# Layer starts of a four-layer graph kernel: first rows and values in banks of their own, transposes of two blocks first, accumulator banks reordered

## The chip, the core and the metric

The kernel runs on one core of one Trainium2 chip. The metric is device time in microseconds (us). Before the change it is 2941.99 us, the median of 3 runs (2940.94 to 2942.51).

A core has TensorE (PE in the profile, with its weight loads as PEld), VectorE (DVE), ScalarE (ACT), GpSimd (POOL) and SyncE (SP, which here only issues transfers). The engines run side by side and meet through semaphores. Matmul results land in PSUM, which has eight banks of 128 partitions by 512 fp32 values. Everything else lives in SBUF.

## The reference

4096 nodes with 256 features pass through four layers. Each is wrapped in `x = layernorm(x + layer(x, adj))`. The adjacency is symmetric with ones on the diagonal, about 1.6% dense.

```python
# layer 1: additive attention, 4 heads of 64
Wh = (h @ W).reshape(n, heads, d)
e = leaky_relu(s_i[:, None, :] + s_j[None, :, :], 0.2)      # s_i, s_j = Wh . a[:, :d], Wh . a[:, d:]
alpha = softmax(where(adj == 0, -inf, e), axis=1)
out = elu(einsum('ijh,jhd->ihd', alpha, Wh))
# layer 2: multi-head attention, 4 heads of 64
q, k, v = split(x @ Wq + bq), split(x @ Wk + bk), split(x @ Wv + bv)
attn = softmax(q k^T / 8 + (edge.T - 1) * 10000);  ctx = attn @ v
# layer 3: additive attention, one head, slope 0.01, elu(attention @ h)
# layer 4: cosine attention
att = softmax(where(adj > 0, cosine(x Wq^T, x Wk^T), -9e15));  out = 0.5 * att @ x + 0.5 * x
```

## The kernel before

All matmuls are fp32, and an fp32 matmul shows as two PE records. The 4096 query nodes are cut into 8 blocks `b` of QW = 512 (four tiles of 128 each), and the key nodes into 32 tiles `j` of 128 (layer 2: 64 half tiles of 64). The features of all nodes stay in SBUF, in `X`. Layer by layer, each unit (b, j) makes weights of 128 keys by 512 queries, and `sums` multiplies them by the values `V` into accumulators in PSUM. `transposed_block` (L112) turns the four tiles of a block of X by PE into `xT`, two banks of PSUM copied to SBUF.

**Layer 1** (`additive_heads`, L196). With `g = 1 - slope`, exp(leaky_relu(s_i + s_j)) is a factor times max(exp(g (s_i + s_j)), 1). So a unit needs a row of exp(g s_i), repeated on all partitions (`row`), and a column exp(g s_j) (`dst`). ScalarE does Relu(row x dst - 1) for each head (L255), VectorE adds 1 and multiplies by the mask (L256), and the sums (L266) follow two units behind (LAG = 2). The order on PE is written out by hand. At its head (L323 to L332) stand five warm-up matmuls, a product that spreads the vector `a` over all partitions for `attach` (L103, which adds the columns of s_i and s_j to the weights by VectorE), `turn(0)`, `prepare(0)` (L176: `V`, `src` and `dst` of block 0), `first_rows` (L228) and `turn(1)`. `first_rows` makes the first row by PE: four transposes per head of a broadcast column of `src`, each head's bank copied to `row[0]` in SBUF by VectorE or ScalarE in turn (L234). Two of its four banks are those of `side`, the others come from the pool `ga_ps` of two banks. PSUM is split into `ga_ps` (2 banks) and two accumulators `acc` of three banks; the first of them is `side`, used by every `prepare`.

**Layer 2** (`multi_head_attention`, L471). A prologue makes keys and queries (`keys`, L505, L510) and `values` (L517) of all blocks, in the order keys(0), the end of layer 1, then turn(b), values(b-1), keys(b); at the end values(6), `greatest` (L530) and values(7). `greatest` bounds the scores from the largest |q| and |k|; ScalarE's exp uses it as `shift`. The matmuls of `values` take 64 nodes at a time, and put the value halves of two pairs of heads on the lower and the upper 64 partitions of one bank, as `V` wants them (L524). VectorE adds the bias in two operations per block (L527). The prologue has one PSUM pool of eight banks. The main part takes them over: three tiles `p` of two banks for the scores (L578), and two accumulators. There PE, DVE and ACT follow a fixed order: scores, exp (L580), mask (L590), sums (L611) three units behind.

**Layer 3** (`additive_one`, L364) has one head and one column of weights per unit. Here a scheduler orders the engines by the program's order and the engines' readiness. `prepare` (L387) turns a block, makes its values (L176), and for the first two blocks the part of the row by transposes (L400) with a copy. Layer 2's last block is copied out of its accumulators (`kept`, L617) meanwhile. Accumulators of even blocks lie in `gb_pa`, of odd blocks (the last too) in the four banks of `gb_ps`.

**Layer 4** (`cosine_attention`, L779). `weights` multiplies normalised rows (L799, tile `p`), exp and mask follow (L802, L803), and `sums` (L810) add up two units behind. At the layer's start the end of layer 3 is still to come: `take_all` (L421, L424 to L426) empties its last accumulators, `outputs` finishes the rows, and `co.prepare` (L750: L761, L765, L767, L772, L776) makes the normalised rows of the last two blocks. PSUM pools come in the order `co_pz` (2 banks), `co_ps` (2), `co_pa` (4 accumulators), and take over the banks of layer 3 in that order.

Of the kernel before, what the change touches and what calls it, by code (L numbers as in the profile page):

```python
# [9 lines left out]
FP = mybir.dt.float32  # L10
# [18 lines left out]
def kernel(  # L29
# [82 lines left out]
    def transposed_block(sb, bank, b, copies=(nc.vector.tensor_copy, nc.scalar.copy)):  # L112

        xT = sb.tile([P, KC, QW], FP, name="xT")
        for c in range(KC):
            pt = bank()
            for k in range(QB):
                nc.tensor.transpose(pt[:, k * P:(k + 1) * P], X[:, b * QB + k, c * P:(c + 1) * P], ident)  # L118
            copies[c](xT[:, c, :], pt)
        return xT  # L120

# [74 lines left out]
    def additive_heads(a, H, slope, early, narrow, ahead):  # L196
# [7 lines left out]
        with ExitStack() as lay:  # L204
# [20 lines left out]
            def bank():  # L225
                return ps.tile([P, QW], FP, name="g")

            def first_rows():  # L228
                row[0] = rp.tile([P, H, QW], FP, name="row")
                for h in range(H):  # L230
                    pr = bank() if h % 2 else side[:, h, :]
                    for k in range(QB):
                        nc.tensor.transpose(pr[:, k * P:(k + 1) * P], src[:, k, h:h + 1].to_broadcast([P, P]), ident)
                    (nc.scalar.copy if h % 2 else nc.vector.tensor_copy)(row[0][:, h, :], pr)  # L234

            def rows(b, pr):

# [7 lines left out]
                nc.sync.dma_start(row[b].rearrange("p h i -> p (h i)"),  # L245
                                  far.rearrange("h k i -> (h k i)").unsqueeze(0).to_broadcast([P, H * QW]))

            def weights(b, j):
                m = b, j // MJ
                if j % MJ == 0:  # L250
                    mask[m] = mp.tile([P, MJ, QW], I32, name="mask")
                    nc.sync.dma_start(mask[m], edges[:, j:j + MJ, b * QW:(b + 1) * QW])
                z = prob[b, j] = zp.tile([P, H, QW], FP, name="prob")
                for h in range(H):
                    nc.scalar.activation(z[:, h, :], row[b][:, h, :], AF.Relu, bias=-1.0, scale=dst[:, j, h:h + 1])  # L255
                nc.vector.scalar_tensor_tensor(z, z, 1.0, mask[m][:, j % MJ, :].unsqueeze(1).to_broadcast([P, H, QW]),  # L256
                                               OP.add, OP.mult)

# [46 lines left out]
                    k = (j - 19) // 2  # L305
                    scale_row(X[:, b * QB + k, :D], mvs[b], roots[b][1], k)

            def turn(b):
                if b + 2 < NB:
                    load_x(b + 2)  # L310
                busy = (nc.scalar.copy if b == 0 else nc.vector.tensor_copy, nc.scalar.copy)
                xTs[b] = transposed_block(sb, bank, b, busy)

            def prepare(b):
# [5 lines left out]
            units = [(b, j) for b in range(NB) for j in range(NT)]  # L320
            with tc.manual_schedule(engines={mybir.EngineType.PE}):

                side = pa.tile([P, HC + 1, QW], FP, name="acc")  # L323

                for _ in range(5):
                    nc.tensor.matmul(side[:, 1, :P], ones, ones, start=True, stop=True)
                nc.tensor.matmul(side[:, 0, :], ones[:1, :], a_row, start=True, stop=True)
                attach(keep, w_sb, side[:, 0, :], H)
                turn(0)
                prepare(0)  # L330
                first_rows()
                turn(1)  # L332
                for i in range(len(units) + LAG):
                    if i < len(units):
                        b, j = units[i]
                        weights(b, j)
                        if (b, j) == (1, 4 * QB):
                            early()
                        if i % 8 == 4:
                            narrow(prob[b, j][:, 0, :1])  # L340
                    if i >= LAG:
                        b, j = units[i - LAG]
                        sums(b, j)
                        if b:
                            finish(b - 1, j)

                    if i == 0 or i % QB == 3 and 3 + i // QB <= NB:
                        b = 1 if i == 0 else 2 + i // QB
                        if b + 1 < NB:
                            turn(b + 1)  # L350
                        prepare(b)
                        if b == 3:
                            rows(1, bank())
                    if i == (NB - 1) * NT + 20:
                        ahead(bank)
# [8 lines left out]
    def additive_one(w_sb, slope, tail, op, follow):  # L364
# [3 lines left out]
        with ExitStack() as lay:  # L368
# [15 lines left out]
            def bank():  # L384
                return ps.tile([P, QW], FP, name="g")

            def prepare(b):  # L387
                xT = transposed_block(sb, bank, b)
                groups = [(k, 1, bank().rearrange("p (n f) -> p n f", n=1)) for k in range(QB)]
                additive_values(xT, b, groups, w_sb, V, src, dst, 1, slope)  # L390
                part = row[:, b * QW:(b + 1) * QW]
                if b > 1:

                    far = dr.tile([QB, P], FP, name="far")
                    nc.gpsimd.dma_start(far.rearrange("k p -> p k"), src[:, b * QB:(b + 1) * QB, 0])
                    nc.gpsimd.dma_start(part, far.rearrange("k p -> (k p)").unsqueeze(0).to_broadcast([P, QW]))
                    return
                pr = bank()
                for k in range(QB):
                    nc.tensor.transpose(pr[:, k * P:(k + 1) * P], src[:, b * QB + k, :].to_broadcast([P, P]), ident)  # L400
                nc.scalar.copy(part, pr)
# [31 lines left out]
                    layernorm_block(b, mvs[b])  # L433

            def even_bank():
                n = next(turn) % QB
                return pa.tile([P, QW], FP, name=f"acc{n}")

            prepare(0)
            prepare(1)  # L440
            turn = itertools.count()
            units = [(b, j) for b in range(NB) for j in range(NT)]
            for i in range(len(units) + 1):
                if i < len(units):
                    b, j = units[i]
                    weights(b, j)
                    if b == 0 and j % QB == 2 and j // QB + 2 < NB:
                        prepare(j // QB + 2)
                if i:
                    b, j = units[i - 1]  # L450
                    sums(b, j)
                    if (b, j) == (0, 2):
                        tail(bank)
                        follow.start()
                    if b and j % 4 == 0 and j // 4 < QB:
                        outputs(b - 1, j // 4)
                    if b == NB - 1 and j in (6, 10, 14):
                        follow.load_mask(0, (j - 6) // 4, prob[b, j][:, :1])

                    if b == NB - 1 and j % 4 == 2 and j // 4 < NB - 2:  # L460
                        follow.prepare(even_bank, j // 4)
                    if j == NT - 1:
                        take_all(b)
# [7 lines left out]
    def multi_head_attention(w_sb, b_sb, tail, rows_of_den, narrow_edges):  # L471
# [12 lines left out]
        with ExitStack() as lay:  # L484
# [7 lines left out]
            with ExitStack() as pro:  # L492
                wp = pool(pro, "mh_w", 1)
                sb = pool(pro, "mh_in", 3)
                ps = pool(pro, "mh_ps", 8, space=PSUM)
                big = {n: wp.tile([P, NB, KC], FP, name=f"{n}big") for n in "qk"}
                xTs = {0: b_sb["x"]}

# [16 lines left out]
                                                    apply_absolute_value=True)  # L515

                def values(b):  # L517
                    n = QW // d
                    for k in range(0, n, QB):
                        pv = bank().rearrange("p (k f) -> p k f", f=P)  # L520
                        for s in range(QB):
                            for c in range(KC):
                                for r in range(KC):
                                    nc.tensor.matmul(pv[r * d:(r + 1) * d, s, :], xTs[b][:, c, (k + s) * d:(k + s + 1) * d],  # L524
                                                     w_sb["v"][:, c, r * P:(r + 1) * P],
                                                     start=(c == 0), stop=(c == KC - 1))
                        nc.vector.tensor_tensor(V[:, b * n + k:b * n + k + QB, :], pv,  # L527
                                                b_sb["v"].unsqueeze(1).to_broadcast([P, QB, P]), OP.add)

                def greatest():  # L530

# [247 lines left out]
    def cosine_attention(co, tail):  # L779
        MJ = co.MJ  # L780
        T, in_ = co.T, co.pool
        with ExitStack() as lay:
            sb = pool(lay, "co_sb", 3)
            pz = pool(lay, "co_pz", 2, space=PSUM)
            ps = pool(lay, "co_ps", 2, space=PSUM)
            pa = pool(lay, "co_pa", 1, space=PSUM)
            ov = out.rearrange("(t p) d -> p t d", p=P)
            acc, prob, y = {}, {}, {}

# [78 lines left out]
    with ExitStack() as weights1, ExitStack() as den1, ExitStack() as weights3:  # L868
        wp = weights1.enter_context(tc.tile_pool(name="w1", bufs=1, side="right"))

        def early():
# [5 lines left out]
                bm_sb[n] = wp.tile([P, KC], FP, name=f"b{n}_sb")  # L877
                nc.sync.dma_start(bm_sb[n], bias)
            nc.vector.tensor_scalar_mul(bm_sb["q"], bm_sb["q"], (D // 4) ** -0.5)
            bm_sb["v"] = wp.tile([P, P], FP, name="bv_sb")  # L880
            for c in range(KC):
                half = slice(c * P // KC, (c + 1) * P // KC)
                nc.sync.dma_start(bm_sb["v"][half, :], bass.AP(tensor=bv1.tensor, offset=bv1.offset + c * P,
                                                               ap=[[0, P // KC], [1, P]]))
            load_w(w2_sb[:, :, :D], w2, nc.sync)
            attach(wp, w2_sb, spread(wp, a2, [[1, 2 * D]], [P, 2 * D], "a", nc.sync), 1)

# [51 lines left out]
```

## Time and profile before

The profiled execution spans 2938.2 us. Its chain of waits crosses from stage to stage at the following times; busy times of the engines within each stage come from the trace.

| stage | start to end, us | PE busy | DVE busy | ACT busy |
|---|---|---|---|---|
| layer 1 | 0 to 725.30 | 721.88 | 667.10 | 661.79 |
| layer 2, prologue | 725.30 to 819.95 | 93.48 | 43.81 | 31.59 |
| layer 2, main | 819.95 to 1730.22 | 904.42 | 702.41 | 566.17 |
| layer 3 | 1730.22 to 2251.23 | 519.23 | 288.43 | 237.21 |
| layer 4 | 2251.23 to 2938.20 | 676.55 | 240.11 | 171.75 |

Each row gives one stage; the difference between its length and the PE column is the time in which TensorE did nothing. Lines of the chain in order of time read: start in us, length in us, engine, tile, line of the kernel, and how many records. "issue" stands for time in which the profile shows nothing to wait for. A group line reads: line, engine, operation, out<-in with shapes, count, then total busy time and mean ns of one, then idle time before it and what ended it.

Of single kinds of work the trace shows: 16 additions L527 of 128x512, 690 ns each; the values' product L183 at 128x256 with 423 ns and at 128x768 with 954 ns; copies of xT (L119) of 128x512 by VectorE with 683 ns.

### The profile page before, as it was taken

The page shows a single profiled execution, that of the slowest core. Times are in us where ns is not written, and L with a number is a line of the kernel's source. Part 1 is how long each engine was busy: PE and PEld are TensorE (multiplying, and loading weights), DVE is VectorE, ACT ScalarE, POOL GpSimd, SP SyncE. Part 2 cuts the span into 40 slices and gives each one's busy share as a digit, 9 for nine tenths or more (in the row PEclk, how much of TensorE's full clock was granted, in tenths as well). Part 3 has the DMA queues.
Part 4 walks back from the last instruction along what each step waited for, and adds up shares of the span by engine and source line. Part 5 has one row for each costly group of instructions (what it writes and reads, how often), then busy time and mean ns, then how long its engine had stood idle before and what let it go on. Part 6 is the DMA issues. An engine that isn't in the chain of part 4 may idle for free.

```text
span 2938.2 us, 50968 instructions
## 1 busy us (share of the span) xinstructions
PE 2915.6 (99%) x20591; PEld 1564.9 (53%) x20591; DVE 1941.9 (66%) x2488; ACT 1668.5 (57%) x2606; POOL 927.5 (32%) x647
## 2 busy tenths in 40 slices
PE   9999999999999999999999999999999999999998
PEld 5333333333643333333333358888887777777776
DVE  8899999997467777877877865555555333333333
ACT  7899999997356666666666654444444222222222
POOL 1000010100078888888889860000000000000000
PEclk9999999999999999999999999999999999999999
DMA  7566666654068888889889876444442333333331
GB/s 202 104 136 142 136 137 139 142 128 80 1 146 191 184 182 190 179 186 192 176 189 187 179 160 139 151 151 151 154 132 53 50 58 58 58 58 58 58 58 29
DMA packets 207166, 374.91 MB, mean 128 GB/s; under 512 B 15073, under 2 KB 90833, under 8 KB 206034
## 3 DMA queue, kind: packets, MB, share of 16 engines
q0 software_dynamic: 102304, 177.77, 38.2%
q1 hardware_dynamic: 104352, 193.62, 20.2%
q8 instruction: 161, 2.64, 0.4%
q14 instruction: 75, 0.61, 0.1%
q10 hardware_dynamic: 274, 0.26, 0.0%
HBM read 317.00 MB, written 21.04 MB: 115 GB/s over the span
## 4 chain that ended last, share of the span: by engine, by line
PE 97%; DVE 2%; ACT 1%; issue 0%; DVEq 0%; ACTq 0%
PE acc L266 23%; PE acc L810 15%; PE p L578 14%; PE acc L611 14%; PE acc L418 8%; PE g L418 7%; PE p L799 4%; PE g L799 3%; PE g L510 2%; PE g L176 1%; PE g L524 1%; PE acc L176 1%; PE g L118 1%; PE acc L761 1%; DVE s L138 1%; DVE prob L590 1%
## 5 line engine op out<-in xcount | busy, mean ns | idle before, releaser
L590 DVE TENSOR_TENSOR prob<-p,mask 128x1024 f32<-128x1024 f32 x512 | 623.0, 1223 | 202.5 <-ACT p L580 198.3
L580 ACT ACTIVATE p<-p,shift 128x1024 f32<-128x1024 f32 x512 | 556.2, 1088 | 333.8 <-PE p L578 333.0
L266 PE MATMUL acc<-prob,V 128*32 128x512 f32 x6144 | 663.8, 592 | 0.0
L597 POOL TENSOR_TENSOR den<-den,prob 128x1024 f32<-128x1024 f32 x248 | 612.8, 2471 | 80.4 <-DVE prob L590 66.0
L255 ACT ACTIVATE prob<-row,dst 128x512 f32<-128x512 f32 x1024 | 635.5, 711 | 0.1
L256 DVE SCALAR_TENSOR_TENSOR prob<-prob,mask 128x2048 f32<-128x2048 f32 x256 | 582.8, 2287 | 25.1 <-ACT prob L255 21.5
L578 PE MATMUL p<-qT,kT 64*64 64x512 f32 x4096 | 532.7, 590 | 6.6 <-DVE prob L590 5.8
L611 PE MATMUL acc<-prob,V 64*64 64x512 f32 x4096 | 531.5, 589 | 0.0
L810 PE MATMUL acc<-X,prob 128*128 128x257 f32 x2048 | 485.7, 380 | 0.0
L810 PEld LDWEIGHTS acc<-X,prob 128*128 128x128 f32 x2048 | 388.5, 190 | 162.0 <-issue 114.7
L803 DVE TENSOR_TENSOR prob<-prob,mask 128x512 f32<-128x512 f32 x256 | 176.4, 691 | 420.1 <-ACT prob L802 418.9
L266 PEld LDWEIGHTS acc<-prob,V 128*32 128x32 f32 x6144 | 197.4, 110 | 451.6 <-issue 433.5
L91 POOL COPY tick<-prob 128x1 f32<-128x1 f32 x35 | 41.8, 1193 | 1016.8 <-DVE prob L256 643.7
L410 ACT ACTIVATE e<-row,dst 128x512 f32<-128x512 f32 x256 | 184.1, 721 | 235.4 <-DVE prob L412 208.4
L611 PEld LDWEIGHTS acc<-prob,V 64*64 64x64 f32 x4096 | 155.9, 133 | 285.3 <-issue 278.1
L578 PEld LDWEIGHTS p<-qT,kT 64*64 64x64 f32 x4096 | 153.7, 133 | 288.3 <-issue 260.6
L412 DVE SCALAR_TENSOR_TENSOR prob<-e,mask 128x512 f32<-128x512 f32 x256 | 176.8, 691 | 174.2 <-PE acc L418 94.0
L748 POOL DMA_DIRECT2D mask<-in_adjT x64 | 47.4, 741 | 641.1 <-DVE prob L803 507.5
L802 ACT ACTIVATE prob<-p 128x512 f32<-128x512 f32 x144 | 85.8, 596 | 256.9 <-PE p L799 242.9
L603 POOL DMA_DIRECT2D den<-prob x240 | 221.1, 921 | 24.2 <-DVE prob L590 20.3
L418 PE MATMUL g<-V,prob 128*128 128x257 f32 x1024 | 226.6, 380 | 0.0
L418 PE MATMUL acc<-V,prob 128*128 128x257 f32 x1024 | 225.1, 380 | 0.0
(151 smaller groups left out, 1962.4 us busy)
## 6 DMA issues: line engine op xcount, KB each, us to landing
mask<-in_adjT SPq DMA_DIRECT2D x256, 512.0 KB
den<-prob POOLq DMA_DIRECT2D x240, 512.0 KB, 5.3
mask<-edges SPq DMA_DIRECT2D x256, 128.0 KB
mask<-in_adjT POOLq DMA_DIRECT2D x64, 512.0 KB, 5.7
edges<-in_adj POOLq DMA_DIRECT2D x32, 512.0 KB, 9.4
den<-prob SPq DMA_DIRECT2D x16, 512.0 KB
row<-far SPq DMA_DIRECT2D x7, 1024.0 KB
X<-in_x SPq DMA_DIRECT2D x7, 512.0 KB
```

The source lines that it names most:

```text
L255: nc.scalar.activation(z[:, h, :], row[b][:, h, :], AF.Relu, bias=-1.0, scale=dst[:, j, h:h + 1])
L256: nc.vector.scalar_tensor_tensor(z, z, 1.0, mask[m][:, j % MJ, :].unsqueeze(1).to_broadcast([P, H, QW]), OP.add, OP.mult)
L266: nc.tensor.matmul(acc[b][h * G:(h + 1) * G, n, :], part, prob[b, j][:, h, :], start=(j == 0), stop=(j == NT - 1))
L418: nc.tensor.matmul(acc[b][k][:, :D + 1], prob[b, j][:, k * P:(k + 1) * P], V[:, j, :], start=(j == 0), stop=(j == NT - 1))
L578: nc.tensor.matmul(p[c * d:(c + 1) * d, r, :], kT[half, c, j * d:(j + 1) * d], qT[half, c, cols], start=True, stop=True)
L580: nc.scalar.activation(p, p, AF.Exp, bias=shift)
L590: nc.vector.tensor_tensor(z, p, mask[m][:, j % MJ, :].unsqueeze(1).to_broadcast([P, KC, QW]), OP.mult)
L597: nc.gpsimd.tensor_tensor(to, to, flat, OP.add)
L603: nc.gpsimd.dma_start(to, flat, accum_op=OP.add)
L611: nc.tensor.matmul(acc[b][c][r * d:(r + 1) * d, :], V[half, j, r * d:(r + 1) * d], prob[b, j][half, r, :], start=(j == 0), stop=(j == NH - 1))
L799: nc.tensor.matmul(p, T[:, 0, j * P:(j + 1) * P], T[:, 1, cols], start=True, stop=True)
L810: nc.tensor.matmul(acc[b][k], prob[b, j][:, k * P:(k + 1) * P], X[:, j, :], start=(j == 0), stop=(j == NT - 1))
```

## The change

Four edits at the places where one stage starts.

1. **Layer 1's head.** Two warm-up matmuls come before the product of `a`, and two behind `turn(0)`. A second accumulator, `over`, is taken first. The four heads of the first row are transposed into four banks of their own (one of the pool and three of `over`), and the Relus of the first unit read them in PSUM; the copies to `row[0]` come behind them (`keep_rows`). `turn(1)` uses two banks of `side`, and both its copies go to VectorE. `transposed_block` now writes both banks' transposes ahead of both copies.
2. **Layer 2's values.** Whole tiles of 128 nodes by 256 columns, in a pool of their own with two banks, and eight additions per block, of 64 partitions by 2x128, put the parts where `V` wants them. Six banks remain for the rest. The bias is spread over all partitions as a whole row.
3. **Layer 3's start.** The transposes of blocks 0 and 1 come ahead of both `prepare`s.
4. **Layer 4's banks.** The accumulators are taken first, so that they lie on `gb_ps`' banks and the tiles of `p` on `gb_pa`'s.

```diff
     def transposed_block(sb, bank, b, ...):
         xT = sb.tile([P, KC, QW], FP, name="xT")
-        for c in range(KC):
-            pt = bank()
+        pts = [bank() for _ in range(KC)]
+        for c, pt in enumerate(pts):
             for k in range(QB):
                 nc.tensor.transpose(pt[:, k * P:(k + 1) * P], X[:, b * QB + k, c * P:(c + 1) * P], ident)
+        for c, pt in enumerate(pts):
             copies[c](xT[:, c, :], pt)
...
-            def first_rows():
+            def first_rows(banks):
                 row[0] = rp.tile([P, H, QW], FP, name="row")
                 for h in range(H):
-                    pr = bank() if h % 2 else side[:, h, :]
                     for k in range(QB):
-                        nc.tensor.transpose(pr[:, k * P:(k + 1) * P], src[:, k, h:h + 1].to_broadcast([P, P]), ident)
-                    (nc.scalar.copy if h % 2 else nc.vector.tensor_copy)(row[0][:, h, :], pr)
+                        nc.tensor.transpose(banks[h][:, k * P:(k + 1) * P],
+                                            src[:, k, h:h + 1].to_broadcast([P, P]), ident)
+
+            def keep_rows(banks):
+                for h in range(H):
+                    (nc.vector.tensor_copy if h % 2 else nc.scalar.copy)(row[0][:, h, :], banks[h])
...
-            def weights(b, j):
+            def weights(b, j, rows=None):
...
                 for h in range(H):
-                    nc.scalar.activation(z[:, h, :], row[b][:, h, :], AF.Relu, bias=-1.0, scale=dst[:, j, h:h + 1])
+                    r = rows[h] if rows else row[b][:, h, :]
+                    nc.scalar.activation(z[:, h, :], r, AF.Relu, bias=-1.0, scale=dst[:, j, h:h + 1])
+                if rows:
+                    keep_rows(rows)
...
-                busy = (nc.scalar.copy if b == 0 else nc.vector.tensor_copy, nc.scalar.copy)
+                busy = (nc.scalar.copy if b == 0 else nc.vector.tensor_copy,
+                        nc.vector.tensor_copy if b == 1 else nc.scalar.copy)
...
+                over = pa.tile([P, HC + 1, QW], FP, name="acc")
                 side = pa.tile([P, HC + 1, QW], FP, name="acc")
-                for _ in range(5):
-                    nc.tensor.matmul(side[:, 1, :P], ones, ones, start=True, stop=True)
+                warm(2)                       # n matmuls of ones into over[:, 0, :P]
                 nc.tensor.matmul(side[:, 0, :], ones[:1, :], a_row, start=True, stop=True)
                 attach(keep, w_sb, side[:, 0, :], H)
                 turn(0)
+                warm(2)
                 prepare(0)
-                first_rows()
-                turn(1)
+                banks = [bank()] + [over[:, h, :] for h in range(H - 1)]
+                first_rows(banks)
+                free = iter([side[:, 0, :], side[:, 1, :]])
+                turn(1, lambda: next(free))
...
-            prepare(0)
-            prepare(1)
+            for b, xT in enumerate([turn(0), turn(1)]):      # layer 3
+                prepare(b, xT)
...
-                ps = pool(pro, "mh_ps", 8, space=PSUM)
+                ps = pool(pro, "mh_ps", 6, space=PSUM)
+                pv2 = pool(pro, "mh_pv", 2, space=PSUM)
...
                 def values(b):
-                    n = QW // d
-                    for k in range(0, n, QB):
-                        pv = bank().rearrange("p (k f) -> p k f", f=P)
-                        for s in range(QB):
+                    for k in range(0, QB, KC):
+                        pv = pv2.tile([P, KC, D], FP, name="pv")
+                        for s in range(KC):
                             for c in range(KC):
-                                for r in range(KC):
-                                    nc.tensor.matmul(pv[r * d:(r + 1) * d, s, :], xTs[b][:, c, (k + s) * d:(k + s + 1) * d],
-                                                     w_sb["v"][:, c, r * P:(r + 1) * P], ...)
-                        nc.vector.tensor_tensor(V[:, b * n + k:b * n + k + QB, :], pv,
-                                                b_sb["v"].unsqueeze(1).to_broadcast([P, QB, P]), OP.add)
+                                nc.tensor.matmul(pv[:, s, :], xTs[b][:, c, (k + s) * P:(k + s + 1) * P],
+                                                 w_sb["v"][:, c, :], ...)
+                        j = 2 * (b * QB + k)
+                        for n in range(2):
+                            for r in range(2):
+                                nc.vector.tensor_tensor(V[r * d:(r + 1) * d, j + n:j + n + 2 * KC - 1:2, :],
+                                                        pv[n * d:(n + 1) * d, :, r * P:(r + 1) * P],
+                                                        b_sb["v"][n * d:(n + 1) * d, r * P:(r + 1) * P].unsqueeze(1)
+                                                        .to_broadcast([d, KC, P]), OP.add)
...
             sb = pool(lay, "co_sb", 3)                        # layer 4
+            pa = pool(lay, "co_pa", 1, space=PSUM)
             pz = pool(lay, "co_pz", 2, space=PSUM)
             ps = pool(lay, "co_ps", 2, space=PSUM)
-            pa = pool(lay, "co_pa", 1, space=PSUM)
...
-            bm_sb["v"] = wp.tile([P, P], FP, name="bv_sb")    # and two transfers of half the bias
+            bm_sb["v"] = spread(wp, bv1, [[1, D]], [P, D], "bv_sb", nc.sync)
```

## The prediction

> **What bounds the kernel now.** I read the page's totals first, then its chain of waits, then the chain again in order of time around each edited place. The totals and the chain's shares:
>
> ```profile
> PE 2915.6 (99%) x20591; PEld 1564.9 (53%) x20591; DVE 1941.9 (66%) x2488; ACT 1668.5 (57%) x2606; POOL 927.5 (32%) x647
> ...
> PE 97%; DVE 2%; ACT 1%; issue 0%; DVEq 0%; ACTq 0%
> ```
>
> TensorE is busy for 2915.6 of 2938.2 us, so only 22.6 us of its idle time can be won, plus whatever makes its own work shorter. The change must therefore be judged at the few places where the chain leaves PE. The head of layer 1 is one (columns: start, length, engine, tile, line):
>
> ```profile
> 3.56 2.00 PE acc L327 x2
> ...
> 7.46 0.37 issue
> 7.84 4.72 PE acc L176 x12
> ...
> 15.55 1.33 ACT prob L255 x2
> 16.89 0.47 ACT row L234
> 17.36 1.23 ACT prob L255 x2
> 18.59 0.48 ACT xT L119
> ...
> 23.34 5.29 PE acc L266 x48
> ```
>
> ScalarE alternates row copies and Relus, an xT copy waits behind them, and the first two units (x48) begin only at 23.34. The step from layer 2's values to its first scores is the second place:
>
> ```profile
> 815.51 3.67 PE g L524 x64
> ...
> 819.20 0.70 DVE V L527
> ...
> 819.95 1.13 PE p L578 x8
> ```
>
> PE waits 0.77 us (819.18 to 819.95) for the last addition to V, because its bank is one of those that the first scores take. The starts of layers 3 and 4 are the others:
>
> ```profile
> 1730.25 0.69 DVE kept L617
> 1730.94 0.61 DVE xT L119
> ...
> 1731.59 3.76 PE g L176 x16
> ...
> 1736.41 0.70 DVE xT L119
> ```
>
> ```profile
> 2253.96 0.41 DVE o L426
> ...
> 2254.51 1.95 PE p L799 x4
> ...
> 2267.63 1.24 DVE rows L772
> ...
> 2269.01 1.06 PE g L776 x8
> ```
>
> Layer 3 starts with one block's transposes, waits for their copy, and does so again for the next block. In layer 4 the first product p waits 3.3 us for the previous layer's last o, and later PE waits for the scaled rows.
>
> **What the Trainium skill says.** "TensorE: Matmul & The Clock Gate", Part 2, has matmuls stay in program order, with only weight loads pulled ahead. The trace agrees: at 2251.23 one waiting p holds up transposes behind it that need nothing of it. Its Part 1 says that the array starts at half clock and gets the full one after about 3.4 us of sustained work, in a window that runs free of the kernel. The records agree about the halving (L176 takes 0.44 us a record until about 11.2 us and 0.22 after), while the page's clock row shows nine tenths or more in every slice. "TensorEngine Tiling (Array Packing)", Key Properties, says a change of tiling mode drains the engine. The trace fits: L118's eight transposes take 1.02 us behind the 32-column L266 (28.62) and 0.87 elsewhere; L510's sixteen records take 7.06 us behind the 64-column L524, against 6.87 at their 0.429 us rate.
>
> **Head of layer 1.** Two warm-up matmuls at 0.5 us (2.50/5) in place of five let the a_row product start near 2.1 instead of 3.56. Its reader, the three DVE operations of 0.7 us that prep(0) now waits for, then ends near 6.4. X's first block becomes the limit: the DMA rows of the first 20 us show 0.8 MB moved by 4.5 us, which is that block and the weights. Transposes from 4.4 (1.9 us), then two warm-ups, give prep(0) at 7.4, not 7.84: 0.4 earlier (0 to 0.5). Sixteen row transposes at 0.11 us then run without a wait, the next two blocks' turns follow, and prep(1) ends near 20.9 instead of 23.34. But ScalarE and VectorE now set the start: ScalarE does the four Relus straight from PSUM, two row copies (0.58) and unit 1's Relus; VectorE does a row copy (0.69) and the product of unit 0 (2.29 by its row, L256) to 20.5. The first unit can start near 21.2, 2.1 earlier. The second product is queued behind an xT copy (0.65) and V's two products (0.95 and 0.42, L183) that come before it on VectorE, so it ends near 25.2 where before it ended at 24.33. Two units (2.65 each) end at 27.8 instead of 28.62. I take -0.8; the ends are +0.5 (the second product later still) and -2.5 (the full clock comes a window earlier, worth half of 3.4 us).
>
> **Values of layer 2.** Per block, 64 records of 64-column weights (3.64 to 3.67 us in the chain) become 16 records of 256 columns. L176's 264-column records take 0.2225 us, so 256 take 0.216, and the block 3.45: -0.19, eight times -1.5. The following keys no longer come out of column tiling: 7.06 - 6.87 = 0.19 a block at most, 0 at least; I take half of it for six blocks, -0.6. The evacuation goes from two additions of 128x512 (0.69) to eight of 64 partitions by 256 elements. No row has that shape; the nearest, V at 128x256, takes 0.42, and I take that, with 0.69 as the dear end. Each block then costs VectorE 3.4 instead of 1.4 us beside 11.4 us of PE, which hides it. After the last block it doesn't lie beside PE: two banks hold values, and sixteen additions queue ahead of the first prob. At 0.42 the last ends near 821.0; the first exp ends at about the same time, so VectorE isn't late. The first scores stop waiting for V, as values have their own two banks: -0.77. With six banks left, the first keys' second bank waits for kept's copy of layer 1: +0.3. Bias load: one transfer for two, read a layer later, nothing. Layer 2: -2.6 (-1.2 to -3.6).
>
> **Layer 3's start.** All sixteen transposes (1.74 us) go first and run beside the copies of kept and xT that PE now waits for. The waits 1730.94-1731.59 and 1736.4-1737.25 shrink to about one of them: first sums end 1741.9 instead of 1743.3, the next block at about 1744.0 instead of 1745.4. I take -1.35 (-0.7 to -2.0); the doubled first prob (1.37 where others take 0.69) I leave as it is.
>
> **Layer 4's banks.** The accumulators, needed last, move onto the banks that layer 3 releases last; p gets banks that its last block doesn't hold. p, its transposes and the next p start at 2251.23, not 2254.51. That is not 3.3 us won, for the sums need prob, and rows still come through VectorE: the o's, three normalisations and L772 end near 2268.0 instead of 2268.87, with one p and one sum done before them instead of after (0.43 + 0.87). Sums of unit 3 end at 2270.35 instead of 2272.66: -2.3 (-0.9 to -3.3).
>
> All else keeps its order on a PE that is busy, and costs nothing. Sum: -0.8 - 2.6 - 1.35 - 2.3 = -7.05, so 2941.99 - 7.05 = 2934.9 us.
>
> **Rivals.** *Given back:* each start ends in a wait on VectorE, whose work is not less; only the values' rate (1.5), their wait (0.77) and some 0.75 of layer 3 stay: 2939.0. For it: all four chains pass through VectorE after PE. Against: the layers behind are PE-bound, so an earlier start carries on to the end. *More than summed:* the clock opens earlier (1.7), every mode change costs its full 0.19 (another 0.7), and layers 3 and 4 reach their far ends (0.65 + 1.0): 2930.9. For it: real work is now gapless from 4.4 us. Against: the window's phase is not the kernel's. *Slower:* the narrow additions take 0.69 each. The sixteen last then end near 825, 3 to 4 us behind the first exp; the second bank of the last values waits 1.6 for its predecessor's; the head loses 0.5; nothing of layers 3 and 4 remains; the rate gives 1.5: 2941.99 + 4 + 1.6 + 0.5 - 1.5 = 2946.6. Against: 256 elements on all partitions already cost only 0.42, and half the partitions shouldn't cost more.
>
> **Numbers.** Forecast 0.58, given back 0.21, more 0.16, slower 0.05. The range runs from the larger gain to the given-back case: 2930.8 to 2938.9, leaving the slow case and tails out. A difference of 0.2% is 5.9 us, to 2936.1: the forecast lies 1.2 below it, so about 0.04 of its chance falls above. The slow case lies 1.3 below the upper bound of 2947.9, but its costs would rather come larger than smaller: I put 0.04 of it above. Faster 0.54 + 0.16 = 0.70, slower 0.04, the rest 0.26.
>
> **What would show it.** V's additions near 0.42 and the last over before 821; L590's first wait on ACT rather than on V; keys after values at 6.9 to 7.0; values 3.45 a block; sums of unit 1 directly behind unit 0 or a gap of over a microsecond between them; layer 3 with sixteen transposes in a row and one xT wait; L799's wait for o gone, with rows the last to come. I am wrong if VectorE's additions cost 0.69, if the gap in the head exceeds 3 us, or if the layers' stretches, clear of their starts, differ in length.

## The result and the profile after

The changed kernel takes 2932.93 us, the median of 6 runs (2931.16 to 2935.99), against 2941.11 for the kernel before (6 runs, 2939.06 to 2942.51). The ratio is 0.9973, with a 95% interval of 0.996 to 0.9985: about 8 us less. The forecast was 2934.9, 7.05 us less than the time then known. The sum came out nearly right. The terms of the values and of layer 4 did not, and about 1.6 of the 8 us came from two things that stood in none of its terms: an earlier full clock in the head (0.9), and a clash of two engines that didn't take place in the profile of the changed kernel (0.7).

The page of the changed kernel, totals and chain by engine:

```profile
PE 2911.7 (99%) x20205; PEld 1559.8 (53%) x20205; DVE 1956.5 (67%) x2537; ACT 1668.4 (57%) x2605; POOL 925.4 (32%) x647
...
PE 97%; DVE 2%; ACT 1%; issue 0%; DVEq 0%; ACTq 0%
```

PE's busy time fell by 3.9 us (2915.6 to 2911.7) and the span by 8.1 (2938.2 to 2930.1), so 4.2 us is idle time won. What PE waited for, in total us, times and longest, first in the kernel before and then in the changed one:

```profile
PE p L578 <- DVE prob L590: 5.8, 8, 1.0
PE p L799 <- DVE o L426: 2.0, 1, 2.0
PE g L176 <- DVE xT L119: 1.3, 3, 0.4
...
PE p L578 <- DVE V L527: 0.8, 1, 0.8
```

```profile
PE p L604 <- DVE prob L616: 5.9, 8, 1.0
PE acc L274 <- DVE prob L264: 1.2, 1, 1.2
...
PE acc L177 <- DVE xT L120: 0.5, 1, 0.5
...
PE g L802 <- DVE rows L798: 0.3, 1, 0.3
```

The waits for o, for xT at the start of layer 3 and for V are gone. In layer 1's head two have come, 1.2 us for a product of VectorE and 0.5 for xT; they take the place of four shorter ones there, 1.9 us together, that the excerpt leaves out.

To see where the 8 us lie I cut the span at PE's own records: first key product, first score, last sums of layers 2 and 3 (its start plus its length at the steady rate), end. The boundaries in the table ahead of the prediction come from the chain, which leaves PE when the *first* accumulator of a last sum is complete; PE then still has the other three to do. Layer 3 ends at 2252.35 on PE, not at 2251.23. Each entry is worked out from record starts in the trace of one execution, so it has the chance of that execution in it.

| us | before | changed | difference | predicted |
|---|---|---|---|---|
| layer 1, to the first key product | 725.23 | 723.60 | -1.63 | -0.8 |
| layer 2's prologue, to the first score | 94.72 | 91.81 | -2.91 | -2.6 |
| layer 2, main part | 910.04 | 910.13 | +0.09 | 0 |
| layer 3 | 522.36 | 520.42 | -1.94 | -1.35 |
| layer 4 | 685.86 | 684.17 | -1.69 | -2.3 |

The head of the changed kernel in its chain of waits:

```profile
7.42 4.07 PE acc L177 x12
11.49 0.89 PE g L177 x4
...
17.38 2.15 DVE prob L264
19.53 0.56 issue
20.09 0.33 DVE xT L120
20.42 0.27 issue
20.69 1.06 DVE V L184 x2
21.75 0.13 issue
21.89 2.29 DVE prob L264
...
24.22 2.78 PE acc L274 x24
```

The first product is over at 19.53, but VectorE then makes an xT copy and V's two products before the second product (21.89 to 24.18), for which unit 1 waits. That is the queue that the prediction described, each step about a microsecond earlier. The step to the first scores of layer 2:

```profile
733.33 3.46 PE pv L546 x16
736.78 6.87 PE g L532 x16
...
811.78 1.96 PE pv L546 x8
...
817.30 0.43 DVE V L551
...
817.76 1.24 DVE prob L616
...
819.04 1.09 PE p L604 x8
```

Values take 3.46 us, the keys behind them 6.87. The last addition to V ends at 817.73, and the first prob starts right behind it, when the first exp is also over. Layer 4:

```profile
2246.12 1.72 PE p L826 x4
...
2260.78 1.24 DVE rows L798
...
2262.16 1.07 PE g L802 x8
```

p follows layer 3's sums without a gap, and the rows are what PE waits for, 0.3 us.

### The profile page after: what moved, and what is told of

Read it like the earlier page. It is cut to its first block, busy times and chain, and to the rows that moved or that the text cites. A ratio compares the mean times of both kernels' runs of the same rounds, so it can differ in the third digit from the quotient of the medians.

```text
span 2930.1 us, 50252 instructions
## 1 busy us (share of the span) xinstructions
PE 2911.7 (99%) x20205; PEld 1559.8 (53%) x20205; DVE 1956.5 (67%) x2537; ACT 1668.4 (57%) x2605; POOL 925.4 (32%) x647
## 4 chain that ended last, share of the span: by engine, by line
PE 97%; DVE 2%; ACT 1%; issue 0%; DVEq 0%; ACTq 0%
PE acc L274 23%; PE acc L837 15%; PE p L604 14%; PE acc L637 14%; PE acc L438 8%; PE g L438 8%; PE p L826 4%; PE g L826 3%; PE g L532 2%; PE g L177 1%; PE pv L546 1%; PE acc L787 1%; PE g L118 1%; PE acc L177 1%; DVE s L139 1%; DVE prob L616 1%
```

## The experiments

### Each part alone

Four kernels take one part of the change each.

```diff
# h_only: the kernel before with part 1 (layer 1's head)
+                banks = [bank()] + [over[:, h, :] for h in range(H - 1)]
+                first_rows(banks)
...
# v_only: with part 2 (values, 6 + 2 banks, bias)
+                pv2 = pool(pro, "mh_pv", 2, space=PSUM)
...
# t_only: with part 3 (layer 3's transposes)
+            for b, xT in enumerate([turn(0), turn(1)]):
+                prepare(b, xT)
...
# b_only: with part 4 (layer 4's banks)
+            pa = pool(lay, "co_pa", 1, space=PSUM)
             pz = pool(lay, "co_pz", 2, space=PSUM)
             ps = pool(lay, "co_ps", 2, space=PSUM)
```

h_only:


> Only the head of layer 1 is changed (and transposed_block's order of copies). Theory (the parts add up): layer 1 ends about 1.6 us earlier than before (before: 725.30), the rest keeps its length to within 0.2, so the span falls by 1.6 to about 2936.6. Rival (a head's gain is returned at the next wait on VectorE): the end of layer 1 moves, the first score of layer 2 doesn't, and the span stays within 0.5 us of 2938.2. The array reaches its full clock near 9.8 if the shorter warm-up sets it, near 11.2 if not.

v_only:


> Only layer 2's values, the banks of its prologue and the bias load are changed. Theory: values 3.46 us a block, keys behind values 6.87 (the drain on leaving the 64-column mode gone whole), no wait for V before the first score, one wait of about 0.3 for kept in the first keys: prologue 2.9 us shorter, span about 2935.3. Rival (half of the drain remains, as predicted): keys 6.97, prologue 2.3 shorter, span 2935.9. Rival (VectorE gives it back): first prob waits for V's additions and layer 2's main part is longer than 910.3 by what the prologue lost.

t_only:


> Only layer 3's start (two blocks transposed first, both banks' transposes before both copies). Theory: from the end of layer 2 to the last sums of layer 3 on PE 1.9 us less than before (before: 1730.22 to 2252.5, 522.3), span about 2936.3. Rival (1.35, as predicted, the rest of the gain in the changed kernel coming from its earlier parts): 520.9, span 2936.9.

b_only:


> Only layer 4's banks. Theory (the wait of p for the last o was 2.0 us by the trace's list of waits, not 3.3, since PE still ran sums until 2252.5): from there to the last sum 1.6 us less, span about 2936.6. Rival (2.3 as predicted, some of it lost in the changed kernel to its other parts): span 2935.9. Rival (given back at the scaled rows): the wait for rows grows by about 2 us and the span stays within 0.5 of 2938.2.

Measured in one profiled execution each, with the same cuts (the last column is the profiled span):

| us | layer 1 | prologue | layer 2 | layer 3 | layer 4 | span |
|---|---|---|---|---|---|---|
| before | 725.23 | 94.72 | 910.04 | 522.36 | 685.86 | 2938.2 |
| h_only | 723.76 | **95.12** | 910.00 | 522.43 | 685.68 | 2937.0 |
| v_only | 725.20 | **91.41** | 909.83 | 522.10 | 685.76 | 2934.3 |
| t_only | 725.23 | 94.72 | 910.06 | **522.46** | 685.69 | 2938.2 |
| b_only | **724.04** | 94.72 | 910.06 | 522.34 | **684.60** | 2935.8 |
| changed | 723.60 | 91.81 | 910.13 | 520.42 | 684.17 | 2930.1 |

Values and banks act in their own stage. The values win 3.31 us, not 2.9: the 0.40 that the changed kernel gives back in its first keys is not the price of six banks, for h_only, with eight, has it too (95.12), and v_only, with six, hasn't. It comes with the head: by the code its second accumulator puts the last block of layer 1 on the other three banks, and in h_only's chain the first keys stand behind the copies out of them:

```profile
723.90 0.59 ACT kept L279
...
725.88 5.42 PE g L528 x12
```

The banks of layer 4 win 1.26 alone and 1.69 together. That isn't an interplay of the parts: 60 us into the layer both kernels are 1.75 us ahead of the kernel before. The rest parts between 350 and 510 us into the layer, where traces with the same code there differ by up to 0.5; its cause is open. Two entries fit no theory. Layer 3's part alone wins nothing. And b_only, which has the old head, finishes layer 1 1.19 us earlier than the kernel before. Both needed a cause that is not in the edit.

Timed on one chip, one run each, the four took 2938.86, 2936.13, 2939.99 and 2937.63 us in this order, beside 2938.86 for the kernel before. Fourteen runs of the kernel before on another chip range from 2938.74 to 2941.36, so such single times can't carry differences of a microsecond, and the argument rests on the lengths of the stages in the profiles.

### The clock in the head

w_five puts the warm-up matmuls back where they were:

```diff
-                warm(2)
+                warm(5)
                 nc.tensor.matmul(side[:, 0, :], ones[:1, :], a_row, ...)
...
                 turn(0)
-                warm(2)
                 prepare(0)
```

> The changed kernel with five warm-up matmuls ahead of the product of a and none behind the first turn, as before. Theory (the two warm-ups behind turn(0) and the earlier start of real work bring the full clock a step earlier): values of block 0 start near 7.8, the full clock comes near 11 us, the first product on VectorE ends near 20.5 and layer 1 ends about 1 us later than in the changed kernel (723.7). Rival (the clock's window runs free and the time of full clock is chance): full clock anywhere between 9 and 11.5, layer 1 later by 0.4 only.

And both kernels were profiled once more as they are.

> The kernel before again. Theory: full clock anywhere from 9 to 11.5, and the end of layer 1 with it between 723.7 and 724.9; layer 3 522.4. Rival: 11.49 and 724.9 as in its first profile.

> The changed kernel again, to see what chance does. Theory: the full clock of the head comes at another time than 9.75, layer 1's end moves with it by about half the difference, and layer 3 takes either 520.4 or 522.5 by whether GpSimd's join starts before or behind the fourth prob. Ratio 0.9973 within 0.001. Rival: both places repeat the first profile to 0.1 us.

The products of block 0's values show the step to full clock: a record's length drops from 647 to 386 ns, and the distance between two starts from 0.44 to 0.22 us. The five records around the step, in the profile of before and of the changed kernel (shortest, median and longest ns, first and last start):

```profile
L176 PE MATMUL acc<-w_sb,xT x5: 386/387/647, 10.6 to 11.9; 128*128 128x264 f32 x5
```

```profile
L177 PE MATMUL acc<-w_sb,xT x5: 386/617/647, 8.4 to 10.0; 128*128 128x264 f32 x5
```

I read the start of the first short record in every trace. The last column is the start of the first key product less half of that time, since by these distances a microsecond ahead of the step does half the work.

| kernel | head | full clock, us | layer 1, us | less half |
|---|---|---|---|---|
| before | old | 11.49 | 725.23 | 719.5 |
| before_again | old | 11.44 | 725.19 | 719.5 |
| v_only | old | 11.45 | 725.20 | 719.5 |
| v_pair | old | 9.27 | 724.12 | 719.5 |
| before_gate (below) | old | 12.18 | 725.92 | 719.8 |
| t_only | old | 11.48 | 725.23 | 719.5 |
| b_only | old | 9.18 | 724.04 | 719.5 |
| changed | new | 9.75 | 723.60 | 718.7 |
| after_again | new | 8.05 | 722.79 | 718.8 |
| n_split (below) | new | 8.20 | 722.98 | 718.9 |
| h_only | new | 9.22 | 723.76 | 719.2 |
| w_five | new, old warm-ups | 9.73 | 723.79 | 718.9 |

Six of the seven rows with the old head agree to 0.1 us once the clock is taken off: b_only's 1.19 us was the clock alone. The same program can have its step at different times (8.05 and 9.75), so chance has a share. For the changed kernel the expectation came out: layer 1 0.8 us earlier with a step 1.7 us earlier, layer 3 at 520.44. The kernel before repeated its step (11.44 and 11.49), as the rival had it, but not its layer 3, which took 523.09 (see the clash below). The kernels that share its head scatter from 9.18 to 12.18.

At the same clock time the new head is worth 719.5 - 718.7 = 0.8 us, of which 0.4 goes back in the first keys of layer 2. The other 0.9 of the 1.63 is half of the 1.74 us by which the step came earlier in that profile. The expectation for w_five, full clock near 11 and layer 1 a microsecond later, failed: 9.73, and 0.2 later.

The differences of 0.1 to 0.4 within the two heads go with the start of block 0's values. In h_only it came 0.8 us late, since the transposes waited 0.6 us for X to land; in before_gate 0.8 late, behind ScalarE's copy of xT; in n_split 0.2 late, since the product of `a` waited for its row to land. In w_five it came 0.4 late, at 7.84 in place of 7.42, and there the five warm-ups are the reason. So the place of the warm-ups is worth about 0.2, but n_split, with the changed kernel's own head, lost as much to the landing of a transfer.

Whether the new order brings the step forward on the whole stays open: every trace with the new head has it before 9.8 (the last version below too, at 9.43), five of the seven old ones at 11.4 or later, but two of these at 9.2.

### The drain between modes

The old values' matmuls have weights of 64 columns, the keys' and the transposes' have 128 (128*64 and 128*128 in the records). Passing from one form to the other is what the expectation calls a change of mode. v_pair leaves the values' form as it was and makes two blocks' values in a row:

```diff
-                        if b < NB - 1:
-                            values(b - 1)
+                        if b < NB - 1 and b % 2 == 0:
+                            values(b - 2)
+                            values(b - 1)
                         keys(b)
```

> The kernel before with the values of two blocks made back to back (values 0 and 1 ahead of keys 2, and so on), so that layer 2's prologue goes into and out of the 64-column mode half as often. Theory (each change of mode costs about 0.2 us, once on the way in and once on the way out): 128 records of values take about 7.1 us, only the keys behind values take 7.06 and the others 6.87, and the prologue is 1.0 to 1.2 us shorter. Rival (the 64-column records are slower by themselves): 128 records take 7.28 us and keys behind values 7.06, and only the three keys without values win 0.19 each, 0.57 in all.

```profile
734.04 7.13 PE g L510 x16
741.17 0.87 PE g L118 x8
742.05 7.14 PE g L524 x128
749.18 7.08 PE g L510 x16
```

The 128 records take 7.14 us where twice 64 take 7.28. If the second half costs what the work costs, one passage into the mode takes 0.14 and the work itself 3.50, against 3.46 in the new form: by this sum nearly all of what the new values win is the change of mode, not the rate. By record starts, the transposes ahead of values take 0.97 us in the kernel before and 0.87 in v_only, the keys behind 6.97 and 6.87. The places around the mode thus cost 0.10 + 0.14 + 0.10 = 0.34 of the 0.38 us that a block gets shorter (11.58 to 11.20 in the chain). That part of the theory holds. The rest missed. Keys without values ahead took 6.97 too: they stand behind a wait for xT, and in v_only the one block of keys behind such a wait takes 6.97 as well. And the prologue became 1.1 us *longer* (95.83). In the three blocks without values, keys stand 1.63, 1.42 and 1.42 us behind the start of the transposes, instead of 0.87, waiting for ScalarE's copy of xT. Values between turn and keys hide that copy.

### The narrow additions

n_split doubles their number:

```diff
-    nc.vector.tensor_tensor(V[r * d:(r + 1) * d, j + n:j + n + 2 * KC - 1:2, :], pv[n * d:(n + 1) * d, :, ...], ...)
+    for s in range(KC):
+        nc.vector.tensor_tensor(V[r * d:(r + 1) * d, j + n + 2 * s, :], pv[n * d:(n + 1) * d, s, ...], ...)
```

> The changed kernel with each of the eight additions per block split in two of 64 partitions by 128 elements, so sixteen. Theory (cost per addition is a fixed part of about 0.16 plus 0.26 per 256 elements, so 0.29 each): VectorE 1.3 us more a block, hidden in the prologue, but the last block's additions end about 1.2 us later and hold up the first prob, since they end at the same time as the first exp: layer 2's main part starts 1 to 1.5 later, the span is 1.2 longer. Rival (the first prob doesn't depend on V's additions): the span is the same to 0.3 us.

The group of additions in n_split, and then the changed kernel's from the view of one line (shortest, median and longest ns):

```profile
L552 DVE TENSOR_TENSOR V<-pv,bv_sb 64x128 f32<-64x128 f32 x128 | 32.1, 284 | 6.0 <-PE pv L546 4.8
```

```profile
L551 DVE TENSOR_TENSOR V<-pv,bv_sb x64: 407/422/428, 735.5 to 817.3; 64x256 f32<-64x256 f32 x64
```

284 ns for half the width of 422: each addition has some 146 ns that don't shrink with it. The prologue became 1.12 us longer (92.93 against 91.81): the values' two banks came free late, 0.56 us at block 1 and 0.28 at each of the last two places, and VectorE reached the first prob another 0.4 later (2.74 us after the first score, where the changed kernel has 2.35). From the first key to the first prob that is 1.5 us, and the span, once 0.6 us of an earlier clock is taken off, is 1.3 longer. The forecast 1.2 came out, but by another route: nearly all of it is the two banks, which the expectation had hidden in the prologue, and the 0.4 at the first prob left the main part as long as it was (within 0.1). So dearer additions do cost time, as the prediction feared; at 422 ns the last one ends together with the exp, and no such wait is seen.

### Layer 3: a clash of VectorE and GpSimd

Layer 3 takes 520.4 us in the changed kernel but 522.6 in w_five, with the same code there. The timelines part at the fourth prob. The changed kernel, then w_five (start, length, engine, line, operation):

```profile
1737.66 0.69 DVE L432 SCALAR_TENSOR_TENSOR prob<-e,mask 128x512 f32<-128x512 f32 x1 [1.14 <-PE acc L438]
1738.09 2.49 POOL L646 TENSOR_TENSOR den<-den 128x1024 f32<-128x1024 f32 x1 [8.32 <-DMA den<-prob]
```

```profile
1737.79 2.34 POOL L645 TENSOR_TENSOR den<-den 128x1024 f32<-128x1024 f32 x1 [7.80 <-DMA den<-prob]
1737.88 2.81 DVE L431 SCALAR_TENSOR_TENSOR prob<-e,mask 128x512 f32<-128x512 f32 x1 [1.14 <-PE acc L437]
```

GpSimd's join of layer 2's row sums starts when a transfer lands. If it starts first, the prob ends only after it and takes 2.81 us; if prob starts first, it takes 0.69. In w_five 0.09 us decides. PE feels it through the next copy of xT, which stands behind the prob on VectorE; in w_five and t_only PE waits 1.9 us for that copy, and in the changed kernel not at all. t_only's list of waits has it:

```profile
PE g L177 <- DVE xT L120: 1.9, 1, 1.9
```

Nine traces side by side (us from the end of layer 2's sums; v_only and b_only, left out, look like before):

| kernel | join starts | fourth prob starts | it takes | layer 3 |
|---|---|---|---|---|
| v_pair | 11.17 | 13.34 | 0.73 | 521.74 |
| before | 11.81 | 13.33 | 1.37 | 522.36 |
| h_only | 11.92 | 13.33 | 1.48 | 522.43 |
| before_again | 12.52 | 13.34 | 2.08 | 523.09 |
| t_only | 12.07 | 12.12 | 2.84 | 522.46 |
| w_five | 12.05 | 12.13 | 2.81 | 522.55 |
| n_split | 12.24 | 12.13 | 0.69 | 520.47 |
| changed | 12.55 | 12.13 | 0.69 | 520.42 |
| after_again | 12.70 | 12.13 | 0.69 | 520.44 |

In the old order the join always comes first, and the later it comes the longer the prob. In every trace where it comes first, the two left out included, the prob ends 0.55 us behind the join's end. It works the other way too: in n_split, where the prob starts 0.11 us ahead, it is the join that becomes longer, 2.79 for 2.35, so this isn't the prob waiting for what the join makes. The new order brings the prob forward by 1.2 us, onto the moment at which the join starts. To test it, the join is made to wait for that prob:

```diff
             join_sums(b, 1, nc.gpsimd)
-            join_sums(b, 2, nc.gpsimd)
+            with behind(seen):              # seen: one column of prob[0, 3]
+                join_sums(b, 2, nc.gpsimd)
```

> The kernel before, with only GpSimd's last join of row sums put behind the fourth prob of layer 3. Theory: that prob takes 0.7 instead of 1.37, and layer 3 is 0.7 shorter, 521.7; the rest of the 1.9 us by which the changed kernel's layer 3 can be shorter, 1.2, is then what transposing two blocks first is worth. Rival (all of the gain is from the clash): 520.4 here too.

```profile
1744.06 0.69 DVE L412 SCALAR_TENSOR_TENSOR prob<-e,mask 128x512 f32<-128x512 f32 x1 [1.57 <-PE acc L418]
...
1744.97 2.34 POOL L620 TENSOR_TENSOR den<-den 128x1024 f32<-128x1024 f32 x1
```

The prob takes 0.69 again. The next prob starts 19.59 us after layer 2's end, where the kernel before has 20.27: 0.68 less, as expected. In the changed kernel it starts at 18.38, so 1.21 us is what the transposes of two blocks first are worth. All of layer 3 took 521.97, 0.3 more than expected. The loss lies in its last block: a VectorE operation of 128x8 elements (L770) takes 0.44 us there instead of 0.16, and PE then waits 0.3 for the scaled rows. Meanwhile GpSimd issues a transfer of the mask; in the kernel before, that issue begins 0.6 us ahead of the operation, here 0.3. Only the two kernels with the gated join, this one and the next, show it. That the two engines clash here too is likely, but not tested, and why the gate moves GpSimd is open.

### A version with both repairs

```diff
-                    (nc.vector.tensor_copy if h % 2 else nc.scalar.copy)(row[0][:, h, :], banks[h])
+                    (nc.vector.tensor_copy if h == 1 else nc.scalar.copy)(row[0][:, h, :], banks[h])
...
-                    if i == 0 or i % QB == 3 and 3 + i // QB <= NB:
-                        b = 1 if i == 0 else 2 + i // QB
+                    if i == 1 or i % QB == 3 and 3 + i // QB <= NB:
+                        b = 1 if i == 1 else 2 + i // QB
```

With these and the join behind the fourth prob, on top of the changed kernel:

> The changed kernel with three more edits: the last head's first row copied by ScalarE in place of VectorE; prepare(1) issued behind the weights of unit 1; and GpSimd's last join of layer 2's row sums made to start behind the fourth prob of layer 3 (it then can't run into it). Theory: unit 1's product is what PE waits for in the head (1.2 to 1.5 us), so unit 1 ends 1.0 to 1.4 earlier at the same time of full clock; and VectorE's fourth prob, stretched to 2.8 us in some runs by GpSimd reading at the same time, always takes 0.7, so layer 3 takes 520.4 us each time. Ratio to before about 0.9965, and lower than the changed kernel's. Rival (VectorE is behind by all its work, the wait moves to unit 2; and the stretch comes from something else): unit 2 waits instead, layer 3 stays at 520.4 or 522.5 by chance.

```profile
20.25 5.35 PE acc L274 x48
25.60 1.02 PE g L118 x8
```

The first two units run without a gap, and no wait moved to unit 2. Layer 1 ends at 722.20 with the full clock at 9.43; less half of that, 717.5, which is 1.2 us less than the changed kernel's 718.7, as expected. Layer 3 took 520.88, with the fourth prob at 0.69 and 0.4 us again lost in the last block, where the same small operation takes 0.44 again. The time is 2931.51 us (7 runs), a ratio of 0.9971 (0.996 to 0.9983), beside 2932.10 (8 runs) and 0.9972 (0.9962 to 0.9982) for the changed kernel on the same chip. The repair of the head shows in the trace; in the time the two can't be told apart.

## Why the prediction was right, and where it wasn't

- **Head, -0.8.** Right at the same clock, 0.8, and by the steps described: start at 7.42 (7.4 said; 7.42 to 8.21 in the traces with this head, by when transfers land), second product queued behind V's. Its times came a microsecond too late, mostly because the full clock came at 9.75 and not at 11.2, where the prediction had put it from the kernel before (11.49 by record starts). That was named, as an end of the range; what wasn't seen is that kernels with the old head have this scatter too, so that one profile can't serve as the measure of the head.
- **Values, -2.6.** Measured -3.31 alone. The size of the first term was right (3.64 to 3.46 a block), its cause mostly not: the prediction called it the rate, and v_pair puts 0.14 of the 0.18 down to the change of mode. The sum still came out, because the old stretch of 3.64 us had that change in it. The term that was too small is the keys' drain: the prediction took half of 0.19 a block, and the whole of it went, 7.06 to 6.87 in the chain. That a change of mode drains the engine (the Trainium skill, "TensorEngine Tiling (Array Packing)", Key Properties) agrees with v_pair, which puts 0.14 us on the way in. The +0.3 in the first keys was right in size (0.40), wrong in cause: it belongs to the head's accumulators, not to six banks.
- **The additions.** 0.42 us was taken and 422 ns measured. The last ended together with the first exp, as worked out, and the 4 us of the slow rival didn't come.
- **Layer 3, -1.35.** Right in its mechanism and nearly in size: the transposes give 1.2. The other 0.7 of the measured 1.94 is the doubled prob (the fourth, not the first), which the prediction saw (1.37 against 0.69) and left as it is. It isn't fixed: it depends on when GpSimd's join starts, and in t_only and w_five the new order ran into it and lost the whole gain. That the changed kernel's profile has it on the good side is luck.
- **Layer 4, -2.3.** The term was mis-sized: "waits 3.3 us" took the chain's boundary, 2251.23, as the end of PE's work. PE still ran sums until 2252.35, and the list of waits says 2.0. Of that, 1.69 was won over the layer, 1.75 at its start; the wait for rows there stayed at 0.2 to 0.3. Its own pieces (0.87, and 0.43 + 0.87) also make 2.17, not 2.3.
- **The sum.** -7.05 was said, -8.1 in the profiles. Without the 0.9 of the earlier clock and the 0.7 of the clash, 6.5 is left for the four edits: a little less than said, not more. No rival came true as a whole. Of "more than summed" the earlier clock came in half, and the keys' full drain, but not layer 4's far end; "given back" is what happens in layer 3 on some runs.

## What to carry to other kernels

The chain of waits here left PE when the piece that released the next one was complete, 1.1 us before PE was idle: take the length of a wait from the engine's idle time, never from the distance between two pieces of the chain. Before an operation is moved forward by a microsecond, look at what else starts in that microsecond on an engine that shares its memory port. And when one edit alone doesn't give what it gives together with others, compare an untouched stage first: here b_only's untouched head showed the clock's 1.2 us, and two kernels with the same layer 3 the clash.

## What the runs showed of the hardware

- VectorE's prob, an operation with two SBUF inputs, and GpSimd's join held each other up for a whole instruction: 0.69 us became 2.81 when the join had started 0.09 us before, and GpSimd's 2.35 became 2.79 in n_split when the prob had started 0.11 us before. The Trainium skill ("SBUF — State Buffer", "SBUF: two separate sides") says of such a pair that whichever starts first holds the shared port for its whole instruction; the traces agree. The copy of xT, out of PSUM, ran beside the join at its usual 0.68.
- The step to full clock came between 8.05 and 12.18 us in runs of the two heads, and at 8.05 and 9.75 in one and the same kernel; each microsecond is worth half a one at the end of layer 1.
- PE can also fall back. In v_pair the granted clock was 0.50 from 2256 to 2258 us, shortly behind the 2.0 us in which PE waited for o at the start of layer 4; eight transposes took 1.71 us there in place of 0.87, and the layer 687.47. None of the other six traces with that wait shows it, nor any of the six with the new banks, which haven't the wait. Whether the new banks guard against it is not shown.
- An addition of 64 partitions by 256 elements takes as long as V's product on 128 partitions by 256 (0.42 us both); half the width takes 0.28.
